# A cross-attention block on one core: output-projection products 1 and 7 split once more into 128x128 products, and the work of the other engines redistributed

## The chip, the cores and the metric

The kernel runs on 1 core of one Trainium2 chip. The metric is the time of one execution on the device in microseconds (us); the median of several runs is compared. Names of the engines in the profile: PE is TensorE (PEld its weight loads), DVE is VectorE, ACT is ScalarE, POOL is GpSimd, SP is SyncE, which issues most transfers (SPq is its queue). Each engine works off its own instructions strictly in the order of the program, and waits where an operand or a buffer is not ready.

## What is computed

A cross-attention block with adaptive layer norms, all in float32: 16 batches of 1024 query rows and 64 context rows, 512 features, 16 heads of 32. Cut to what matters:

```
ss    = silu(cond) @ W_ss + b_ss               # one scale and one shift per batch
xq    = (1 + scale_q) * layernorm(x)   + shift_q
xkv   = (1 + scale_kv) * layernorm(ctx) + shift_kv
q     = xq @ Wq + bq;   k, v = split(xkv @ Wkv + bkv)
attn  = softmax(q k^T / sqrt(32))              # per head, over 64 context rows
out   = x + (attn v) @ Wp + bp
```

## The kernel before, in words

The 1024 query rows of each batch make two tiles of 512 rows, 32 tiles in all (`NB`), numbered through. The context of all batches is projected once, at the start, as two groups "A" and "B" of 512 rows. The order of every step is written out by hand: a start, a loop `for i in range(3, NB - 2)` (L1587 to L1704), and an end. One loop body holds work of five tiles at once: scores of tile i, the softmax's rest and the mix of a = i-1, the output projection of b = i-2 and a, the query projection of n = i+1, and the features of f = i+2, i+3 and i+4.

**The steps of one tile.** `load_x` brings 512 rows; `q_stats` (L315) takes mean and variance of each row on VectorE (bn_stats and bn_aggr), four row blocks a tile; `q_scale` makes 1/std on ScalarE and POOL; `hidden` normalises on ScalarE (L327); `turn` (L352) transposes 32x32 blocks on VectorE and `move` (L373) brings them to their partitions by 16 transfers of 64 KB; `scale_features` applies scale and shift on ScalarE (L442).

**Seven products.** Both projections multiply 512x512 by 512x512 with Strassen's scheme in Winograd's form: seven products of halves (numbers 1 to 7; 256x256 by 256x256 here, each four matmuls of 128 columns by 256) in place of eight, with sums of halves made beforehand on POOL (`feature_sums` L474, `row_sum` L1046) and the results added up in two PSUM banks and by VectorE (`query_added` L647, `added` L1095). Product 1, 6, 5 and 3 gather in one bank and 2 or 7 and 4 in the other; each is read before the next is added, so the products of a bank follow each other with a reader in between. For the query projection of tiles 4 to 30 products 1 and 7 are split once more: `quarter_products` (L585) multiplies seven pairs of 128x128 quarters, four (`first`) and then three, with differences of quarters made on POOL (`feature_quarters` L578), a copy by ScalarE (`quarter_copies` L614) and three sums by VectorE between the two parts (`quarter_adds` L618). The sums of weight quarters are made once.

**Softmax.** `score_products` (L731) writes the scores of 32 context rows (half z) into two PSUM tiles of two banks each. The tag "s" has two such buffers, so both halves of a tile's scores and the mix of another tile (L919) take the same four banks in turn. `maximum` (L754) reduces a bank pair on VectorE, `copied` (L763) copies it to SBUF on ScalarE, `maxima` (L789) joins the halves and spreads the maximum over the partitions by a VectorE transpose, `subtract` (L795) takes it off on POOL, and `weights` (L803) exponentiates on ScalarE. So that the mix can use 64 context rows per matmul, half the blocks of 32 partitions must change places between the two halves: `swapped` (L810) moves two of the four by transfer, and `again` (L815) exponentiates the other two once more from the scores. `total` (L851) adds the two halves on POOL, `row_total` (L861) sums the rows on VectorE. `inverse_rows` (L875) takes the reciprocals and brings them by way of DRAM into an order from which `spread_rows` (L886) spreads them on VectorE with a 2048-wide transpose. `mix` (L919) multiplies by the values, and `divided` (L898) multiplies the result in PSUM by the spread reciprocals.

**Output projection.** `biased` (L1019) puts the bias into a bank on ScalarE, `output_seed` (L1035) copies product 1's bank to the other, `product` (L1064) runs one of the seven products, `added` adds to the residual rows and, after products 3 and 4, stores them. Tile 29 alone is projected undivided, by `project` (L971). At the very end tile 31 uses halves of banks of its own.

Of the kernel before, what the change touches and what calls it, by code (L numbers as in the profile page):

```python
# [9 lines left out]
F32 = mybir.dt.float32  # L10
# [10 lines left out]
def cross_attention_block(  # L21
# [166 lines left out]
    def load_projection(again=False):  # L188
        src = w_p.rearrange("(c p) o -> p c o", p=P)
        if again:  # L190
            nc.sync.dma_start(w_p_sb[:, : NC // 2, H // 2 :], src[:, : NC // 2, H // 2 :])
        else:
            nc.sync.dma_start(w_p_sb, src)

    ident = const.tile([P, P], F32, name="ident")
# [67 lines left out]
    def scale_shift(name, off, h, n=1):  # L263
        rows = ssr.pop((name, h))
        pst = pss_tiles[name][1]
        if h == 0:
            ss[name] = const.tile([P, 2 * NC, BW], F32, name=f"ss_{name}")
# [47 lines left out]
    def q_stats(i, ts=range(NT)):  # L315

        if ts[0] == 0:
            q_mv[i] = small.tile([P, NT, 2], F32, tag="mvq", name=f"mvq_{i}")
        for t in ts:
            row_stats(q_mv[i][:, t, :], x_tiles[i][:, t, :])  # L320

# [409 lines left out]
    def score_products(i, z):  # L731
# [13 lines left out]
        if z == 0:  # L745
            m_tiles[i] = small.tile([P, 2, HPC, NJ], F32, tag="m2", name=f"m2_{i}")
# [51 lines left out]

    l_tiles = {}
# [14 lines left out]

    def again(i, g):  # L815
# [7 lines left out]
    def sums(i, z):  # L823
        if z == 0:
            l_tiles[i] = small.tile([P, 2, HPC, NJ], F32, tag="l2", name=f"l2_{i}", bufs=1)
# [35 lines left out]
    def row_total(i):  # L861
        lt_tiles[i] = small.tile([P, HPC, NJ], F32, tag="lt", name=f"lt_{i}", bufs=2)
# [8 lines left out]
    def halves_total(i):  # L871
        lt_tiles[i] = small.tile([P, HPC, NJ], F32, tag="lt", name=f"lt_{i}", bufs=2)
        both(lt_tiles[i].rearrange("p r j -> p (r j)"), l_tiles.pop(i), ALU.add)

    def inverse_rows(i):  # L875
# [3 lines left out]
        v = small.tile([P, NC, NJ], F32, tag="vr", name=f"vr_{i}", bufs=2)  # L879
# [4 lines left out]
        vt_rows[i] = v  # L884

# [125 lines left out]
    def acc_bank(i, n):  # L1011

        if n == 2 and i >= NB - 2:
            return 1 if i == NB - 2 else 3
        return (2 if n in (1, 6, 5, 3) else 3) - (2 if i == NB - 1 else 0)
# [3 lines left out]
    def biased(i, k):  # L1019

        b = b_first if k == 2 else b_diff
        if i == NB - 1 and k == 2:
            z_halves.append(bank(f"pp_{i}_0", 0))
            z_halves.append(ps_s.tile([P, 2, TB], F32, tag="s", name=f"pp_{i}_0b")[:, 0, :])
# [10 lines left out]
    def output_seed(i):  # L1035

        seeded.add((i, 2))
        acc[3] = bank(f"pp_{i}_2", 3)
        nc.scalar.copy(acc[3], acc[2])
# [24 lines left out]
    def product(i, n):  # L1064
# [12 lines left out]
        if n == 2 and (i, 2) not in seeded:  # L1077
            acc[k] = bank(f"pp_{i}_{n}", k)
        for t in range(2):
            for c in range(HC):  # L1080
# [12 lines left out]
                )  # L1093

# [29 lines left out]
    w_k_sums = big.tile([P, 4, HC, HO], F32, tag="big2", name="w_k_sums")  # L1124
    warm = bank("warm", 1)
    for _ in range(WARM):
        nc.tensor.transpose(warm[:, :P], ident, ident)
    load_x("A")
    load_scale_shift("kv", w_ss_kv, 0)
    q_stats("A", (0,))  # L1130
    q_stats("A", (1,))
    q_stats("A", (2,))
    load_scale_shift("kv", w_ss_kv, 1)
    q_stats("A", (3,))
    q_scale("A")
    load_context_weights(1, 0)
    hidden("A", (0,))
    biases()
    load_context_weights(0, 1)
    scale_shift_rows("kv", 0)  # L1140
    scale_shift_taken("kv", 0)
    turned_features("A", 0)
    hidden("A", (2,))
    hidden("A", (1,))
    turned_features("A", 1)
    hidden("A", (3,))
    scale_shift("kv", 2 * NC, 0)
    turned_features("A", 2)
    turned_features("A", 3)
    modulated("A", 0, 1, nc.vector)  # L1150
    load_context_weights(0, 0)
    modulated("A", 0, 0, nc.scalar)
    scale_shift_rows("kv", 1)
    scale_shift_taken("kv", 1)
    load_x(0)
    modulated("A", 0, 0, nc.vector)
    modulated("A", 0, 1, nc.scalar)
    load_scale_shift("q", w_ss_q, 0)
    column_sums("k", w_k_sb, w_k_sums, (0,))
    scale_shift("kv", 2 * NC, 1)  # L1160
    load_scale_shift("q", w_ss_q, 1)
    column_sums("k", w_k_sb, w_k_sums, (1,))
    modulated("A", 1, 0, nc.scalar)
    column_sums("k", w_k_sb, w_k_sums, (2,))
    modulated("A", 1, 0, nc.vector)
    context_product("A", "v", 1)
    context_product("A", "k", 2)
    modulated("A", 1, 1, nc.vector)
    load_x("B")
    modulated("A", 1, 1, nc.scalar)  # L1170
    feature_sums("A", nc.vector, (0,))
    context_product("A", "k", 1)
    feature_sums("A", nc.vector, (1,))
    context_out("A", "k", 1)
    feature_sums("A", nc.vector, (2,))
    q_stats(0, (0,))
    context_out("A", "k", 2)
    context_product("A", "v", 2)
    context_product("A", "k", 6)
    q_stats(0, (1,))  # L1180
    q_stats(0, (2,))
    scale_shift_rows("q", 0)
    q_stats(0, (3,))
    q_scale(0)
    context_out("A", "k", 6)
    feature_sums("A", nc.vector, (3,))
    hidden(0, (1,))
    hidden(0, (2,))
    hidden(0, (0,))
    load_context_weights(1, 1)  # L1190
    load_value_bias()
    w_q_sums = qpool.tile([P, 4, HC, HO], F32, tag="wq", name="w_q_sums")
    context_product("A", "k", 7)
    load_query_weights()
    context_out("A", "k", 7)
# [12 lines left out]
    column_sums("v", w_v_sb, wv_sums, (0,))
# [660 lines left out]
```

## Time and profile before

| | |
|---|---|
| runs | 998.51, 998.59, 996.92 us; median 998.51 |
| profiled execution | 996.92 us, its span 996.9 us |
| granted TensorE clock | 1.000 |
| DMA | 165.77 MB, mean 166 GB/s |
| HBM | 79.47 MB read, 34.60 MB written |

The span runs from the first to the last instruction. Busy shares are shares of the span; a matmul's end is modelled and matmuls overlap, so the pace of TensorE is read from start to next start. In lists of instructions, "x8" are eight instructions: a float32 matmul appears as two passes. "[0.65 <-PE po L936]" says that the engine had been idle for 0.65 us until the named instruction of another engine released it.

### The profile page before, as it was taken

Reading aid. Unit: us, or ns where it says so; the run is one execution under the profiler, and the core shown is the slowest. Engines: PE = TensorE matmul, PEld = TensorE weight load, DVE = VectorE, ACT = ScalarE, POOL = GpSimd, SP = SyncE. Lnnn points to the kernel's source line nnn. Section 1 sums busy time; section 2 is a strip of 40 time slices with the busy share of each in tenths; the row PEclk is TensorE's granted clock in tenths of the full one; section 3 lists DMA queues with packets and bytes.
Section 4 is the critical chain, followed back from the end, with each engine's and each line's share of the span. In section 5 each row is a group of like instructions: output and inputs, shape, how many; then the busy total and the mean of one; then the engine's idle time right before and its main releaser. Section 6 shows DMA issues by size and latency. Waiting matters only on the chain.

```text
span 996.9 us, 20564 instructions
## 1 busy us (share of the span) xinstructions
PE 984.2 (99%) x7465; PEld 760.7 (76%) x7465; DVE 895.6 (90%) x1318; ACT 779.3 (78%) x1165; POOL 895.4 (90%) x690
## 2 busy tenths in 40 slices
PE   7999999999999999999999999999999999999998
PEld 6878777787777877877778778777787787777756
DVE  7696899999999999999999999999999999987786
ACT  3878878888888888888888888888888888876620
POOL 2677899999999999999999999999999999999681
PEclk9999999999999999999999999999999999999999
DMA  9765655555655555566655555665555555544422
GB/s 308 264 165 151 156 164 156 140 165 180 190 181 176 159 165 152 151 182 186 183 176 152 173 145 155 185 188 178 176 150 175 151 154 182 148 132 130 145 85 97
DMA packets 115188, 165.77 MB, mean 166 GB/s; under 512 B 34920, under 2 KB 46464, under 8 KB 113168
## 3 DMA queue, kind: packets, MB, share of 16 engines
q1 hardware_dynamic: 114704, 163.93, 55.2%
q8 instruction: 59, 0.97, 0.4%
q0 software_dynamic: 384, 0.54, 0.2%
q14 instruction: 41, 0.34, 0.1%
HBM read 79.47 MB, written 34.60 MB: 114 GB/s over the span
## 4 chain that ended last, share of the span: by engine, by line
PE 88%; DMA 4%; DVE 3%; SPq 2%; POOL 1%; issue 1%; ACT 0%; DVEq 0%; POOLq 0%
PE pp L1086 36%; PE pq L534 27%; PE pq L605 10%; PE ps L738 6%; PE po L936 5%; PE pk_A L534 1%; PE pk_B L534 1%; DMA w_k_sb<-in_L_xcond_Wkv_dram 1%; DMA r<-in_x_dram 1%; PE pv_B L534 1%; DMA ltd<-lt 1%; DMA V_B<-stage_B 1%; DMA vr<-ltd 0%; POOL sum L858 0%; DVE l L826 0%
## 5 line engine op out<-in xcount | busy, mean ns | idle before, releaser
L797 POOL TENSOR_TENSOR s<-s,mb 128x2048 f32<-128x2048 f32 x64 | 290.6, 4564 | 20.3 <-DVE mb L784 13.4
L1086 PE MATMUL pp<-w_p_sb,ot 128*128 128x256 f32 x740 | 174.8, 379 | 1.1 <-DVE ot L915 1.1
L764 ACT COPY s<-ps 128x1024 f32<-128x1024 f32 x128 | 129.3, 1013 | 46.1 <-PE ps L738 34.0
L755 DVE TRANSPOSE_TENSOR_REDUCE m<-ps 128x32 f32<-128x1024 f32 x128 | 152.4, 1228 | 10.4 <-PE ps L738 9.3
L1086 PEld LDWEIGHTS pp<-w_p_sb,ot 128*128 128x128 f32 x740 | 138.2, 190 | 20.5 <-issue 2.8
L645 ACT ACTIVATE qt<-pq,bias_t 128x256 f32<-128x256 f32 x256 | 107.8, 475 | 48.8 <-PE pq L605 27.7
L858 POOL TENSOR_TENSOR sum<-s,p 128x2048 f32<-128x2048 f32 x30 | 136.5, 4549 | 1.6 <-ACT p L808 1.6
L1116 DVE TENSOR_TENSOR r<-pp,r 128x512 f32<-128x512 f32 x183 | 120.3, 669 | 13.8 <-ACT xt L442 6.8
L534 PE MATMUL pq<-xt,w_q_sums 128*128 128x256 f32 x512 | 123.8, 385 | 0.0
L534 PEld LDWEIGHTS pq<-xt,w_q_sums 128*128 128x128 f32 x512 | 95.0, 190 | 34.6 <-issue 22.6
L1086 PE MATMUL pp<-WT,ot 128*128 128x256 f32 x492 | 118.4, 383 | 0.0
L1086 PE MATMUL pp<-WT,s 128*128 128x256 f32 x488 | 116.1, 380 | 1.3 <-DVE r L1107 0.8
L817 ACT ACTIVATE s<-s 32x2048 f32<-32x2048 f32 x60 | 114.6, 1910 | 1.8 <-DMA p<-s 0.4
L1086 PEld LDWEIGHTS pp<-WT,ot 128*128 128x128 f32 x492 | 90.9, 190 | 19.1 <-issue 4.2
L1086 PEld LDWEIGHTS pp<-WT,s 128*128 128x128 f32 x488 | 88.2, 190 | 13.1 <-POOL s L1056 1.3
L327 ACT ACTIVATE x<-x,rstdq 128x512 f32<-128x512 f32 x128 | 94.8, 807 | 1.0 <-POOL rstdq L304 1.0
L442 ACT ACTIVATE xt<-xt,ss_q 128x512 f32<-128x512 f32 x124 | 94.0, 809 | 1.0 <-DMA xt<-ht 0.7
L915 DVE TENSOR_TENSOR ot<-po,vb 128x1024 f32<-128x1024 f32 x62 | 73.0, 1219 | 17.6 <-PE po L936 17.4
L286 DVE BATCH_NORM_STATS2 bs<-x 128x6 f32<-128x512 f32 x128 | 85.3, 666 | 0.0
L493 POOL TENSOR_TENSOR xt_sums<-xt 128x512 f32<-128x512 f32 x64 | 81.2, 1269 | 2.0 <-DMA x<-in_x_dram 1.3
L357 DVE STREAM_TRANSPOSE ht<-x 128x512 f32<-128x512 f32 x124 | 77.7, 679 | 4.7 <-DMA xt<-ht 2.2
L891 DVE STREAM_TRANSPOSE vb<-vr 128x2048 f32<-128x2048 f32 (+1 forms) x33 | 73.7, 2236 | 4.4 <-DMA vr<-ltd 4.4
(224 smaller groups left out, 1963.8 us busy)
## 6 DMA issues: line engine op xcount, KB each, us to landing
x<-in_x_dram SPq DMA_DIRECT2D x32, 1024.0 KB, 5.3
r<-in_x_dram SPq DMA_DIRECT2D x32, 1024.0 KB, 5.9
xt<-ht SPq DMA_DIRECT2D x488, 64.0 KB, 2.0
out_dram<-r SPq DMA_DIRECT2D x60, 512.0 KB, 4.7
p<-s SPq DMA_DIRECT2D x60, 256.0 KB, 3.8
wss_kv<-in_L_xcond_Wss_kv_dram SPq DMA_DIRECT2D x4, 512.0 KB, 7.2
wss_q<-in_L_xcond_Wss_q_dram SPq DMA_DIRECT2D x4, 512.0 KB, 11.0
vr<-ltd SPq DMA_DIRECT2D x128, 8.0 KB, 1.7
```

Source lines behind the costliest of these rows:

```text
L327: nc.scalar.activation(dst, src, AF.Identity, bias=rstd[:, 1, j : j + 1], scale=rstd[:, 0, j : j + 1])
L442: nc.scalar.activation(xt[:, :, c, :], xt[:, :, c, :], AF.Identity, scale=ss["q"][:, c, b : b + 1], bias=ss["q"][:, NC + c, b : b + 1],)
L534: nc.tensor.matmul(out_, lhsT=lhsT, rhs=rhs, start=new and m == 0 and c == 0, stop=c == HC - 1, skip_group_check=True,)
L605: nc.tensor.matmul(qa["q", k][:, q * P : (q + 1) * P], lhsT=lhsT, rhs=rhs, start=first and q == 0, stop=True, skip_group_check=True,)
L645: nc.scalar.activation(dst, src, AF.Identity, bias=bq_t[:, o : o + 1])
L755: nc.vector.tensor_reduce(m_tiles[i][:, z, 2 * e : 2 * e + 2, :], s_banks[i, z][e].rearrange("p r (j a) -> p r j a", a=32), AX.X, ALU.max, ...
L764: nc.scalar.copy(s_tiles[i, z][:, 2 * e : 2 * e + 2, :], s_banks[i, z][e])
L797: eng.tensor_tensor(s_tiles[i, z], s_tiles[i, z], mb_tiles[i], ALU.subtract)
L817: nc.scalar.activation(s_tiles[i, 0][at + 32 : at + 64], raw_tiles[i][at : at + 32], AF.Exp, scale=SCALE)
L858: nc.gpsimd.tensor_tensor(t, s_tiles[i, 0], s_tiles[i, 1], ALU.add)
L1086: nc.tensor.matmul(to, lhsT=rows[:, c, t * P : (t + 1) * P], rhs=cols[:, c, :], start=n == 2 and (i, 2) not in seeded and t == 0 and c == ...
L1116: nc.vector.tensor_add(r, a, r)
```

## The change

**Split products of the output projection.** Products 1 and 7 of tiles 2 to 30, and product 7 of tile 31, become seven products of 128x128 quarters, in the same way as the query projection's, with new functions:

```diff
+    def inner_biased(i, v):
+
+        k = acc_bank(i, v)
+        acc[k] = bank(f"pp_{i}_{k}", k)
+        nc.scalar.copy(acc[k][:, :HO], inner_bias[v])
+        nc.scalar.copy(acc[k][:, HO:], zero.to_broadcast([P, HO]))
...
+    def inner_quarters(i, v, eng=nc.gpsimd):
...
+        x, tt = inner_rows(i, v), eng.tensor_tensor
+        tt(t[:, 0:2], x[:, 1, 0:2, :], x[:, 0:2, 0, :], ALU.subtract)
+        tt(t[:, 2], x[:, 1, 1, :], t[:, 0], ALU.subtract)
+        tt(t[:, 3], x[:, 0, 1, :], t[:, 2], ALU.subtract)
+
+    def inner_products(i, v, first):
...
+        if first:
+            todo = (
+                (0, w(0, 0), x[:, 0, 0, :]),
+                (2, s(0), t[:, 0]),
+                (1, s(2), t[:, 1]),
+                (3, s(1), t[:, 2]),
+            )
+        else:
+            todo = (
+                (0, w(0, 1), x[:, 0, 1, :]),
+                (2, s(3), x[:, 1, 1, :]),
+                (1, w(1, 1), t[:, 3]),
+            )
...
+    def inner_copies(i, v):
+        a = acc[acc_bank(i, v)].rearrange("p (k e n) -> p k e n", k=2, e=2)
+        nc.scalar.copy(inner_tiles[i, v][:, 0:2], a[:, :, 0, :])
+
+    def inner_adds(i, v):
+
+        a, t, tt = acc[acc_bank(i, v)], inner_tiles[i, v], nc.vector.tensor_tensor
+        both_ = a[:, P : 3 * P].rearrange("p (k n) -> p k n", k=2)
+        tt(t[:, 2], a[:, 3 * P :], t[:, 0], ALU.add)
+        tt(both_, both_, t[:, 2:3].to_broadcast([P, 2, P]), ALU.add)
+        tt(a[:, 3 * P :], a[:, P : 2 * P], t[:, 1], ALU.add)
```

The weight quarters' sums are made once (`inner_weight_sums`), one of them in place, so `load_projection(again=True)` now reads 512 KB back, late in the end, where it read 256 KB earlier in it. Tile 29 uses the seven products too, and `project` is not called any more. Tile 31's query products 1 and 7 are split.

**Softmax.** For tiles 3 to 30 the second half's scores are not copied to SBUF and not lowered by POOL: `lowered` subtracts the maximum on VectorE straight from the score banks, which stay taken until then. For tiles 2 to 29 `exchanged` moves all blocks by six transfers of 256 KB, and `again` is gone. For tiles 2 to 30 the reciprocals are transposed (64 wide), written to DRAM and read back already spread, by four broadcast reads of 256 KB, and `spread_rows` is gone:

```diff
+    def lowered(i, e):
+        rs = slice(2 * e, 2 * e + 2)
+        nc.vector.tensor_tensor(
+            s_tiles[i, 1][:, rs, :], s_banks[i, 1][e], mb_tiles[i][:, rs, :], ALU.subtract
+        )
...
+    def exchanged(i, k):
...
+        t = raw_tiles[i]
+        for g in range(2):
+            lo, hi = slice(64 * g, 64 * g + 32), slice(64 * g + 32, 64 * g + 64)
+            dst, src = ((t[lo], s0[hi]), (t[hi], s1[hi]), (s0[hi], s1[lo]))[k]
+            nc.sync.dma_start(dst, src)
...
+    def reciprocal_rows(i):
...
+        nc.vector.reciprocal(flat, flat)
+        nc.vector.transpose(v.rearrange("p k a -> p (k a)"), flat)
+        nc.sync.dma_start(d.rearrange("k x a -> x k a"), v)
...
+    def read_rows(i, rs=range(HPC)):
...
+        for r in rs:
+            src = vt_rows[i][r // 2].rearrange("(c k j) a -> k c (j a)", c=NC, k=2)
+            src = src[r % 2 : r % 2 + 1].to_broadcast([32, NC, TB])
+            nc.sync.dma_start(vb_tiles[i][32 * r : 32 * r + 32], src)
```

**Row statistics.** For tiles 7 to 31 two of the four row blocks get their mean and variance on ScalarE, in two passes with an accumulator each, and POOL divides the squares by 512:

```diff
+    def q_stats_two(i, ts, last=False):
...
+            nc.scalar.activation(junk, x, AF.Identity, scale=1.0 / H, accum_out=mv[:, t, 0:1])
+            nc.scalar.activation(
+                junk, x, AF.Square, scale=-1.0, bias=mv[:, t, 0:1], accum_out=mv[:, t, 1:2]
+            )
```

**The order.** All of it is written anew. The loop now runs `for i in range(5, NB - 4)`, 23 bodies, and its body starts at another point of the cycle. Its calls in order, with the guards that always hold or hold until the last tiles left out:

```
query_out(i,6); maxima(a); product(i-3,3); scale_features(n,2); quarter_products(i,7,first);
product(i-3,4); scale_features(n,0); lowered(a,0); lowered(a,1); quarter_copies(i,7);
added(i-3,3); quarter_adds(i,7); weights_whole(a,1); mix(b); turn(f,0); subtract(a,0);
added(i-3,4); inner_biased(b,1); weights(a,0); quarter_products(i,7,second); turn(f,1);
feature_quarters(n,1); divided(b,0); inner_quarters(b,1); exchanged(a,0); query_product(i,5);
divided(b,1); inner_products(b,1,first); query_out(i,7); total(a); turn(f,2); load_residual(a);
turn(f,3); q_stats_two(i+3,0); query_added(i,5); inner_copies(b,1); exchanged(a,1);
row_sum(b,0); inner_adds(b,1); query_product(i,4); query_product(i,3); scale_features(n,3);
q_stats_two(i+3,1); query_out(i,3); move(f,0); inner_products(b,1,second); row_sum(b,2);
query_added(i,4); output_seed(b); q_stats(i+3,2); q_stats(i+3,3); score_products(i,0);
copied(i,0,1); row_sum(b,1); q_square_mean(i+3); exchanged(a,2); product(b,2); row_total(a);
maximum(i,0,0); quarter_products(n,1,first); added(b,2); inner_quarters(b,7);
quarter_copies(n,1); move(f,1); reciprocal_rows(a); feature_sums(n,0); maximum(i,0,1);
product(b,6); load_x(i+4); inner_biased(b,7); inner_products(b,7,first); move(f,2);
copied(i,0,0); q_scale(i+3); feature_sums(n,1); quarter_adds(n,1); feature_sums(n,2);
added(b,6); move(f,3); read_rows(a,0:2); score_products(i,1); read_rows(a,2:4);
quarter_products(n,1,second); inner_copies(b,7); product(b,5); feature_sums(n,3);
inner_adds(b,7); hidden(i+3,0); inner_products(b,7,second); query_seed(n); query_product(n,2);
hidden(i+3,3); maximum(i,1,0); feature_quarters(n,7); query_product(n,6); maximum(i,1,1);
added(b,7); hidden(i+3,2); hidden(i+3,1); row_sum(b,3); query_out(n,2); added(b,5);
scale_features(f,1)
```

At the start, the loads are issued in the order context A, x of tile 0, both parts of the scale and shift weights for keys and values, then the key weights of the first half, a half of the value weights and the other key weights (before: context A, the scale and shift weights, the value weights' half, the key weights' halves the other way round, and then x of tile 0), and the first product on TensorE is the key product 1 instead of the value product 1. The tiles 28 to 31 are written out one by one at the end.

A few small tiles lose a buffer or share one with another (`lt`, `vr` and `m2`, the identity matrix's place), and the statistics' scratch and product 7's quarter tile take the place of the spread maximum (tag "spread").

More of the change, by code (lines that the diff above doesn't have):

```diff
@@ L1076, in product @@
         k = acc_bank(i, n)
-        if n == 2 and (i, 2) not in seeded:
+        if n == 2 and (i, 2) not in seeded and k < 4:
             acc[k] = bank(f"pp_{i}_{n}", k)
@@ new lines, in cross_attention_block @@
+    subtract(3, zs=(0,))
+    product(1, 3)
+    weights_whole(3, 1)
+    query_product(4, 5)
+    inner_weight_sums(1)
+    inner_weight_sums(7)
+    quarter_products(4, 7, False)
+    mix(2)
+    feature_quarters(5, 1)
+    q_stats_two(7, (0,))
+    added(1, 4)
+    query_out(4, 7)
+    added(1, 3)
+    query_added(4, 5)
+    query_product(4, 3)
+    query_product(4, 4)
+    divided(2, (0,))
+    q_stats_two(7, (1,))
+    inner_biased(2, 1)
+    inner_quarters(2, 1)
+    weights(3, 0)
+    divided(2, (1,))
@@ new lines, in cross_attention_block @@
+    q_stats_two(31, (0,))
+    quarter_adds(28, 7)
+    turn(30, (0,))
+    product(25, 3)
+    added(25, 3)
+    turn(30, (1,))
+    product(25, 4)
+    turn(30, (2,))
+    quarter_products(28, 7, False)
+    added(25, 4)
+    mix(26)
+    divided(26, (0,))
+    query_product(28, 5)
+    query_out(28, 7)
+    divided(26, (1,))
+    q_stats_two(31, (1,))
+    query_added(28, 5)
+    turn(30, (3,))
+    feature_quarters(29, 1)
+    inner_quarters(26, 1)
+    load_residual(27)
+    inner_biased(26, 1)
@@ new lines, in cross_attention_block @@
+    query_out(30, 6)
+    quarter_adds(30, 7)
+    product(27, 4)
+    added(27, 3)
+    lowered(29, 1)
+    lowered(29, 0)
+    added(27, 4)
+    query_product(30, 5)
+    scale_features(31, (3,))
+    quarter_products(30, 7, False)
+    query_out(30, 7)
+    query_added(30, 5)
+    subtract(29, zs=(0,))
+    weights_whole(29, 1)
+    mix(28)
+    feature_sums(31, nc.gpsimd, (0,))
+    feature_quarters(31, 1)
+    inner_biased(28, 1)
+    weights(29, 0)
+    query_product(30, 3)
+    divided(28, (0,))
@@ L1730, in cross_attention_block @@
+    read_rows(29, (2, 3))
+    quarter_adds(z, 7)
+    weights(y, 1)
+    weights(y, 0)
+    quarter_products(z, 7, False)
+    query_out(z, 7)
+    query_added(z, 5)
+    load_residual(NB - 1)
+    added(y - 2, 4)
+    mix(y - 1)
+    divided(y - 1, (0,))
+    divided(y - 1, (1,))
+    total(y)
     query_product(z, 4)
-    query_added(z, 5)
     query_product(z, 3)
-    product(y - 2, 5)
-    again(y - 1, 1)
+    query_out(z, 3)
+    inner_biased(y - 1, 1)
     query_added(z, 4)
-    added(y - 2, 7)
```

1697 lines of the change are left out of this document (1104 added, 593 removed).

## The prediction

> **What bounds the kernel now.** I read the page, then the busy time by stretches, then each engine's timeline over one tile, then the ends.
>
> ```profile
> span 996.9 us, 20564 instructions
> PE 984.2 (99%) x7465; PEld 760.7 (76%) x7465; DVE 895.6 (90%) x1318; ACT 779.3 (78%) x1165; POOL 895.4 (90%) x690
> ```
> ```profile
> 0.00:25.00 25.00, 18.92 (x158) 16.20 (x159) 17.55 (x49) 9.41 (x24) 7.43 (x13) 1.00 0.95 308
> ...
> 200.00:228.30 28.30, 28.30 (x220) 21.95 (x219) 26.76 (x40) 24.26 (x37) 27.57 (x22) 1.00 0.61 182
> ...
> 960.00:997.00 37.00, 31.68 (x186) 23.18 (x184) 26.98 (x33) 5.12 (x5) 12.41 (x8) 0.99 0.30 108
> ```
> The columns of a stretch are its length, then PE, PEld, DVE, ACT and POOL busy, the granted clock, the DMA share and GB/s. TensorE is never idle in the middle; of its 12.7 us of idle time (996.9 less 984.2) 6.1 lie in the first 25 us and 5.3 in the last 37. So the time moves only by TensorE work taken away, or by new idle time. But POOL with 27.57 and DVE with 26.76 of 28.30 stand right behind it. The timelines give the pace, start to next start, which is shorter than a row's own duration because operations overlap:
>
> ```profile
> 501.05 1.89 PE L534 MATMUL pq<-xt,w_q_sb 128*128 128x256 f32 x8
> ...
> 504.51 0.38 PE L605 MATMUL pq<-xt_sums,w_q_sums 128*128 128x128 f32 x2
> 504.73 0.83 PE L605 MATMUL pq<-t_quarters,w_p_sb 128*128 128x128 f32 x6
> 505.40 1.89 PE L1086 MATMUL pp<-w_p_sb,ot 128*128 128x256 f32 x8
> 507.13 1.89 PE L1086 MATMUL pp<-WT,ot 128*128 128x256 f32 x8
> ...
> 529.57 1.89 PE L534 MATMUL pq<-xt,w_q_sb 128*128 128x256 f32 x8
> ```
> A plain product is 8 passes in 1.73 us (505.40 to 507.13). Four quarter products are 8 passes in 0.89 us (504.51 to 505.40), 0.111 a pass, so seven of them, 14 passes, take 1.56. One tile takes 28.52 us (501.05 to 529.57).
>
> **TensorE's work.** Products 1 and 7 of the output projection are split for tiles 2 to 30 and 2 to 31: 59 in all, 57 of them outside tile 29, each 1.73 less 1.56 = 0.17: 9.5 us. The query products 1 and 7 of tile 31 give 0.3. Tile 29 loses its undivided projection:
>
> ```profile
> 947.68 7.11 PE L974 MATMUL pp<-w_p_sb,ot 128*128 128x512 f32 x16 [0.33 <-PE ps L738]
> 954.72 2.35 PE L947 MATMUL po<-s,V_B 32*32 32x512 f32 x64
> 957.00 7.13 PE L974 MATMUL pp<-w_p_sb,ot 128*128 128x512 f32 x16
> 963.97 3.62 PE L1086 MATMUL pp<-w_p_sb,ot 128*128 128x256 f32 x16
> ```
> That was 7.04 + 6.97 = 14.0; five plain and two split products take 8.65 + 3.12 = 11.8, so 2.2 less. TensorE loses 12.0 us, and a tile of the loop falls from 28.52 to 28.18.
>
> **VectorE.** One tile of its timeline:
>
> ```profile
> 491.72 2.31 DVE L863 TRANSPOSE_TENSOR_REDUCE lt<-sum 128x64 f32<-128x2048 f32 x1
> ...
> 494.89 2.39 DVE L755 TRANSPOSE_TENSOR_REDUCE m<-ps 128x32 f32<-128x1024 f32 x2 [0.27 <-PE ps L738]
> ...
> 501.55 2.31 DVE L784 STREAM_TRANSPOSE mb<-m 128x2048 f32<-128x2048 f32 x1
> 503.79 0.65 DVE L1116 TENSOR_TENSOR r<-pp,r 128x512 f32<-128x512 f32 x1
> 504.36 0.67 DVE L286 BATCH_NORM_STATS2 bs<-x 128x6 f32<-128x512 f32 x1
> ...
> 505.17 0.66 DVE L286 BATCH_NORM_STATS2 bs<-x 128x6 f32<-128x512 f32 x1
> ...
> 506.54 0.28 DVE L622 TENSOR_TENSOR t_quarters<-pq,t_quarters 128x128 f32<-128x128 f32 x1
> ...
> 507.53 2.30 DVE L891 STREAM_TRANSPOSE vb<-vr 128x2048 f32<-128x2048 f32 x1
> 509.75 1.25 DVE L1116 TENSOR_TENSOR r<-pp,r 128x512 f32<-128x512 f32 x2
> 511.65 2.36 DVE L915 TENSOR_TENSOR ot<-po,vb 128x1024 f32<-128x1024 f32 x2 [0.65 <-PE po L936]
> 513.92 2.48 DVE L357 STREAM_TRANSPOSE ht<-x 128x512 f32<-128x512 f32 x4
> ...
> 520.23 2.31 DVE L863 TRANSPOSE_TENSOR_REDUCE lt<-sum 128x64 f32<-128x2048 f32 x1
> ```
> Of the 28.51 from L863 to L863 it waits 0.27 + 0.65 = 0.92 and works at most 27.59. Removed: the spreading of the reciprocals (L891, 2.22) and two of four row statistics (0.81 each). Added: two `lowered`, which read a score bank and an SBUF tile as L915 does (2.27 for two), two `inner_adds`, each like L622 to L624 (0.99), and a 64-wide transpose (L784 does 2048 in 2.24, so 0.1 in proportion, at most 0.3). Sum: 27.59 - 2.22 - 1.62 + 2.27 + 1.98 + 0.1 = 28.1. Against TensorE's 28.18 next to nothing is left, where 0.92 was: this is what decides the change.
>
> The pace matters here. The Trainium skill ("VectorE: DVE Perf Modes", section The DRAIN you can't avoid) says that the next operation does not start until the pipe of the one before is empty. By that rule, the trace disagrees: L1116 lasts 0.65 and L286 starts 0.57 after it.
>
> **The other engines.**
>
> ```profile
> 501.92 0.74 POOL L581 TENSOR_TENSOR t_quarters<-xt_sums 128x256 f32<-128x256 f32 x1
> ...
> 504.01 9.08 POOL L797 TENSOR_TENSOR s<-s,mb 128x2048 f32<-128x2048 f32 x2 [0.27 <-ACT qt L645]
> 513.05 1.28 POOL L1051 TENSOR_TENSOR s<-ot 128x512 f32<-128x512 f32 x1
> ```
> ```profile
> L764 ACT COPY s<-ps 128x1024 f32<-128x1024 f32 x128 | 129.3, 1013 | 46.1 <-PE ps L738 34.0
> L645 ACT ACTIVATE qt<-pq,bias_t 128x256 f32<-128x256 f32 x256 | 107.8, 475 | 48.8 <-PE pq L605 27.7
> L817 ACT ACTIVATE s<-s 32x2048 f32<-32x2048 f32 x60 | 114.6, 1910 | 1.8 <-DMA p<-s 0.4
> L327 ACT ACTIVATE x<-x,rstdq 128x512 f32<-128x512 f32 x128 | 94.8, 807 | 1.0 <-POOL rstdq L304 1.0
> ```
> POOL gives up one subtraction (4.52) and gets two sets of quarter differences (501.92 to 503.74, 1.82 each): 0.9 less with one tiny product. ScalarE drops two score copies (2.0) and the two second exponentials of `again` (3.8), and gets four passes of statistics as long as L327 (3.2; the accumulator is not in the trace, 0 to 0.3 each, I take 0.1) and small copies (0.8): 1.5 less. Neither can become the bound; both keep their order, so the question there is only lateness.
>
> SP and the DMA queues get more:
>
> ```profile
> q1 hardware_dynamic: 114704, 163.93, 55.2%
> ...
> p<-s SPq DMA_DIRECT2D x60, 256.0 KB, 3.8
> ...
> b_p_sb<-in_L_xcond_bp_dram SPq DMA_DIRECT2D x1, 256.0 KB, 6.5
> ```
> Per tile, four more exchanges of 256 KB and four broadcast reads of 256 KB in place of four small ones: 2 MB, 58 MB over the kernel. 163.9 MB take 55.2% of the queue engines, so 222 MB would take 75%: not the bound, but transfers land later. An exchange landed in 3.8 us; a broadcast read of the same size in 6.5, and I take 4 to 6.5. The last exchange waits on SP for POOL's `total`, as `swapped` did; behind it stand feature moves, and what it brings is used a tile later. The reads stand behind 8 feature moves:
>
> ```profile
> 493.56 8.28 SPq L382 DMA_DIRECT2D xt<-ht  x11
> ```
> At 0.75 each these are 6.0, with the other issues 8.5, so the last read lands at most 8.5 + 6.5 = 15.0 after the reciprocals. Its first user, `divided`, comes after 15.5 us of VectorE's queue (three maxima 3.5, two `quarter_adds` and one `inner_adds` 3.0, five residual sums 3.0, `maxima` 2.6, `lowered` 2.3, two transposes 1.2): it fits by 0.5, or by 3 at 4 us a read. `lowered` itself waits for nothing new but `maxima`, ahead of it in the same queue; behind it stand a residual sum and `quarter_adds`, for which TensorE has 2 us more.
>
> **Three tight places of the new loop,** each TensorE against the chain it waits for. (1) The mix takes the score banks only after `lowered`. TensorE does 10.9 us in between (two second halves of a split product, 0.67 each, one first half, 0.89, five plain products, 8.65); VectorE needs 0.27 + 2.4 (two maxima) + 1.2 (two residual sums) + 2.57 (`maxima`) + 2.27 = 8.7. 2.2 are left, or 1.2 with an `inner_adds` in front. (2) From the mix to the first inner products TensorE has 0.67 + 1.73 = 2.4; the chain is 0.16 + 1.2 (`divided`, one half) + 0.82 (the first quarter difference, L581 with its gap) = 2.2. 0.2 are left. (3) The scores need both halves of `query_out` of product 3, 0.2 + 0.84 (two L645, overlapping), while only 0.67 of inner products lie between, where before a whole product of 1.73 did. 0.3 short if all scores wait for both halves, 0 if the first column of scores starts on the first half; I take 0.05 a tile, near the lower end, since the scores walk through the columns one after the other. Over 23 loop bodies this is 1.2 us, with 0 to 7 as its bounds.
>
> **The ends.** At the start 1 MB (x of tile 0) goes ahead of the scale and shift weights:
>
> ```profile
> 10.75 1.07 PE L248 MATMUL ps_kv<-wss_kv,early 128*32 128x128 f32 x28 [0.99 <-DMA wss_kv<-in_L_xcond_Wss_kv_dram]
> ...
> 19.24 3.69 PE L534 MATMUL pk_A<-xk_A,w_k_sb 128*128 128x256 f32 x16 [1.42 <-DMA w_k_sb<-in_L_xcond_Wkv_dram]
> ```
> At 308 GB/s that is 3.4 us on a TensorE that waits for these weights already; but the first key product then needs 4.5 MB ahead of it, as it did before, so it starts again near 19, and only the value product that ran before it comes later: +1.0 (bounds -1 to +3.4). The half of the projection weights that is read again comes before the last mix and has several microseconds of cover. At the end TensorE had 5.3 idle; the last products still hang on the same mix and the same stores, so 0, with bounds of 1.5 either way.
>
> **The sum.** The profiled execution took 996.92 us, as its span does, and is the lowest of the three runs; the median 998.51 is 1.6 above it. 996.9 - 12.0 + 1.2 + 1.0 = 987.1, and 988.7 as a median.
>
> **Rivals.** (a) Short stalls eat most of the gain: 0.2 to 0.4 more per tile at places 2 and 3, over 25 tiles 5 to 10 us: 994 to 999. For it speaks the 0.2 of room; against it, that TensorE shows no idle time in the loop with POOL as full as it is. (b) VectorE becomes the clock, the slower case: it keeps the 0.92 of waits on top of 28.1, 29.0 a tile against 28.18, over 25 tiles +20: 1009. It decides as soon as its waits pass 0.1 to 0.2 a tile; against it, the waits come from VectorE being early for the scores and the mix, and a later VectorE waits less, while place 1 has room for a VectorE one microsecond later. Late reads of the reciprocals would end the same way: 2 us beyond their room put 2 us on each tile. (c) The operations of VectorE do not overlap: 40 instructions in the stretch of 28.30 with about 0.05 of overlap each are 2 us more, 30.1 a tile, +48: 1037. The old tile would then have been 29.6 instead of 28.51, so 1 in 100. This is what the rule of the Trainium skill cited above would make of the change. (d) The split brings no time because the order outside the loop loses what it gives, an end that costs 8 us or more: 997, with only 1 in 25, as the ends hold just 11 us of idle time and are built of the same waits.
>
> **Numbers.** Forecast 0.67 (984 to 993), (a) 0.14, (b) 0.14, (c) 0.01, (d) 0.04. Two in a thousand, 2.0 us, is about what can be told from no change. Faster (below 996.5): 0.67 and two thirds of (a), 0.76; same: the rest of (a) and (d), 0.09; slower: (b) and (c), 0.15. The range takes in the forecast's own bounds and (a): 984 to 1000.
>
> **What would show it.** Right: PE busy near 972, still 99%; a loop tile of 28.2 to 28.3; the split product's seven in 1.56; DVE at 27.6 to 28.1 a tile with waits under 0.5. Place 3 would show as PEld waiting on `qt`, place 2 as PE waiting on POOL's quarter tile, the reads as DVE waiting for a transfer into `vb`. Wrong: a tile of 28.5 or more with PE idle behind DVE, or a start in which TensorE idles over 8 us.

## The result and the profile after

The changed kernel takes 1141.43 us (median of four runs, 1139.02 to 1143.58) against 998.55 before (four runs, 996.92 to 999.48). The ratio is 1.1434, with a 95% interval of 1.1415 to 1.1453. The change makes the kernel 143 us slower; the forecast was 988.7 us, in a range of 984 to 1000.

The page of the profiled execution (1141.46 us): the span, the busy times, the DMA queue, and three rows of the DMA issues (KB each, median us from issue to landing).

```profile
span 1139.7 us, 22368 instructions
...
PE 1027.8 (90%) x7855; PEld 803.5 (71%) x7855; DVE 919.9 (81%) x1457; ACT 717.7 (63%) x1377; POOL 877.7 (77%) x881
...
q1 hardware_dynamic: 123760, 223.02, 72.7%
...
x<-in_x_dram SPq DMA_DIRECT2D x32, 1024.0 KB, 6.5
...
xt<-ht SPq DMA_DIRECT2D x488, 64.0 KB, 4.8
p<-s SPq DMA_DIRECT2D x116, 256.0 KB, 4.8
```

No engine is full any more: TensorE falls from 99% of its span to 90%, and VectorE and POOL fall too. So no engine has become the clock; they wait for one another. Stretches of the same trace (length, PE, PEld, DVE, ACT, POOL busy, granted clock, DMA share, GB/s):

```profile
0.00:25.00 25.00, 18.61 (x147) 16.13 (x148) 16.25 (x53) 9.92 (x28) 5.50 (x12) 0.93 0.94 303
...
300.00:900.00 600.00, 539.41 (x4201) 425.28 (x4200) 501.39 (x781) 396.98 (x779) 479.29 (x493) 0.96 0.79 208
...
1100.00:1139.00 39.00, 34.60 (x247) 28.47 (x232) 29.66 (x45) 7.97 (x13) 18.93 (x17) 1.00 0.36 122
```

In the 600 us of loop TensorE idles 60.6 us and its granted clock is 0.96, where before it was never idle and at 1.00. Taking the start of a tile's first score products as a mark, the 142.8 us (1139.7 less 996.9) lie as follows: up to tile 5 the mark moves from 208.4 to 231.9 (+23.5); from tile 5 to tile 27 the loop takes 726.9 instead of 627.4 (+99.5; 33.04 us a tile instead of 28.52, irregular, 30 to 37); from there to the end 180.9 instead of 161.1 (+19.8).

Who waits for whom, in the groups of waits over the whole kernel (us in total, times, longest):

```profile
ACT xt L459 <- DMA xt<-ht: 122.8, 25, 8.2
DVE t_quarters L639 <- ACT t_quarters L633: 97.4, 22, 8.1
...
PE pq L622 <- DVE pq L641: 66.9, 23, 6.7
```

These three are one chain, once a tile. One stalled tile shows it, first SP's queue, then ScalarE, VectorE and TensorE:

```profile
508.82 0.49 SPq L119 DMA_DIRECT2D x<-in_x_dram  x1
509.35 8.15 SPq L399 DMA_DIRECT2D xt<-ht  x8
517.55 2.04 SPq L948 DMA_DIRECT2D vb<-ltd  x4
```
```profile
519.17 0.81 ACT L459 ACTIVATE xt<-xt,ss_q 128x512 f32<-128x512 f32 x1 [8.11 <-DMA xt<-ht]
...
522.01 0.36 ACT L633 COPY t_quarters<-pq 128x256 f32<-128x256 f32 x1
```
```profile
522.47 0.29 DVE L639 TENSOR_TENSOR t_quarters<-pq,t_quarters 128x128 f32<-128x128 f32 x1 [7.09 <-ACT t_quarters L633]
```
```profile
517.01 1.06 PE L1002 MATMUL po<-p,V_A 64*32 64x512 f32 x16
523.71 0.77 PE L622 MATMUL pq<-xt_sums,w_q_sums 128*128 128x128 f32 x2 [5.64 <-DVE pq L641]
...
525.12 2.67 PE L551 MATMUL pq<-xt,w_q_sums 128*128 128x256 f32 x8
```

The last eight feature moves stand right behind the 1 MB load of x. They take SP 8.15 us, but not evenly. It issues seven of them 0.63 us apart, and the eighth only at 517.00 (the same timeline in two narrower windows):

```profile
509.35 4.36 SPq L399 DMA_DIRECT2D xt<-ht  x7
...
517.00 0.51 SPq L399 DMA_DIRECT2D xt<-ht  x1
```

In all traces of this case SP's transfers carry eight semaphores in turn (a semaphore is the counter by which a landed transfer reports), and no transfer was issued before the one eight places ahead of it, which carried the same semaphore, had landed, wherever the records tell the landing. Eight places ahead of the eighth move stands the x load, which landed at 516.98. Eight places ahead of the second transfer of the third exchange (L852) stands the residual load. SP's own groups of waits from tile 5 to tile 27 show both:

```profile
SPq L852 <- DMA r<-in_x_dram: 54.8, 21, 3.7
SPq L399 <- DMA x<-in_x_dram: 41.9, 22, 3.4
```

Neither wait is there in the loop of the kernel before. The seven moves issued at once land late as well: they come in right behind the load, between 517.27 and 518.33, and the eighth at 518.91.

`scale_features(f, (1,))`, which needs them, is the head of ScalarE's queue for the next body, and behind it stand `query_out(i, 6)` and the copies of a split query product (L633). VectorE's `quarter_adds` waits for those copies, and TensorE for the sums. TensorE then resumes at a lower clock: eight passes take 2.67 us instead of 1.89. The granted clock in that place, by stretches:

```profile
511.00:517.00 6.00, 6.00 (x44) 4.66 (x51) 4.34 (x4) 0.06 (x1) 6.00 (x3) 1.00 0.84 244
517.00:523.70 6.70, 1.07 (x24) 0.17 (x9) 1.09 (x4) 4.53 (x7) 0.01 (x2) 0.97 0.76 174
523.70:526.70 3.00, 2.99 (x10) 2.73 (x11) 3.00 (x5) 2.97 (x5) 1.65 (x3) 0.50 0.72 267
526.70:533.00 6.30, 6.30 (x39) 5.53 (x42) 6.06 (x14) 5.37 (x15) 6.12 (x5) 1.00 0.75 176
```

After a 5.64 us pause the clock is 0.50 for the next 3.0 us, which costs 3.0 × 0.50 = 1.5 us on top of the pause. Over the 600 us, 0.04 of clock is about 24 us and the idle time 60.6: together about 85, and the 18.2 tiles of this stretch are 18.2 × 4.52 = 82 us longer than before. So the loss in the loop is pauses and the low clock behind them.

### The profile page after: what moved, and what is told of

The parts are those of the page before. It is cut to its first block, busy times and chain, and to the rows that moved or that the text cites. A ratio compares the mean times of both kernels' runs of the same rounds, so it can differ in the third digit from the quotient of the medians.

```text
span 1139.7 us, 22368 instructions
## 1 busy us (share of the span) xinstructions
PE 1027.8 (90%) x7855; PEld 803.5 (71%) x7855; DVE 919.9 (81%) x1457; ACT 717.7 (63%) x1377; POOL 877.7 (77%) x881
## 3 DMA queue, kind: packets, MB, share of 16 engines
q1 hardware_dynamic: 123760, 223.02, 72.7%
## 4 chain that ended last, share of the span: by engine, by line
DMA 33%; PE 22%; DVE 15%; ACT 10%; POOL 8%; SPq 8%; issue 4%; DVEq 0%; ACTq 0%; POOLq 0%
DMA x<-in_x_dram 16%; PE pq L551 8%; DMA vb<-ltd 5%; DMA p<-s 5%; POOL sum L902 4%; SPq L399 4%; PE pp L1155 4%; DVE m L772 3%; DMA xt<-ht 3%; ACT xt L459 3%; PE pp L1246 2%; PE pq L622 2%; DVE lt L907 2%; DVE r L1288 2%; DVE ot L981 2%
## 5 line engine op out<-in xcount | busy, mean ns | idle before, releaser
L459 ACT ACTIVATE xt<-xt,ss_q 128x512 f32<-128x512 f32 x124 | 97.3, 810 | 138.0 <-DMA xt<-ht 122.8
L814 POOL TENSOR_TENSOR s<-s,mb 128x2048 f32<-128x2048 f32 x36 | 163.6, 4547 | 12.4 <-DVE mb L801 12.3
L902 POOL TENSOR_TENSOR sum<-s,s 128x2048 f32<-128x2048 f32 x29 | 131.8, 4544 | 2.3 <-ACT s L836 2.2
L1155 PE MATMUL pp<-w_p_sb,ot 128*128 128x256 f32 x524 | 128.2, 388 | 5.1 <-ACT pp L1108 3.8
L1155 PEld LDWEIGHTS pp<-w_p_sb,ot 128*128 128x128 f32 x524 | 95.5, 191 | 38.8 <-ACT pp L1108 23.6
L639 DVE TENSOR_TENSOR t_quarters<-pq,t_quarters 128x128 f32<-128x128 f32 x56 | 15.2, 272 | 99.1 <-ACT t_quarters L633 97.4
L781 ACT COPY s<-ps 128x1024 f32<-128x1024 f32 x72 | 72.1, 1012 | 36.4 <-PE ps L755 24.1
L598 POOL TENSOR_TENSOR t_quarters<-xt 128x256 f32<-128x256 f32 x28 | 20.6, 737 | 91.1 <-DVE pq L641 53.7
L622 PE MATMUL pq<-xt_sums,w_q_sums 128*128 128x128 f32 x112 | 25.9, 316 | 66.9 <-DVE pq L641 66.9
L622 PEld LDWEIGHTS pq<-xt_sums,w_q_sums 128*128 128x128 f32 x112 | 20.8, 207 | 89.9 <-issue 84.1
L801 DVE STREAM_TRANSPOSE mb<-m 128x2048 f32<-128x2048 f32 x32 | 74.0, 2311 | 1.2
```

The lines of the kernel that those rows point to most:

```text
L459: nc.scalar.activation(xt[:, :, c, :], xt[:, :, c, :], AF.Identity, scale=ss["q"][:, c, b : b + 1], bias=ss["q"][:, NC + c, b : b + 1],)
L814: eng.tensor_tensor(s_tiles[i, z], s_tiles[i, z], mb_tiles[i], ALU.subtract)
L902: nc.gpsimd.tensor_tensor(t, s_tiles[i, 0], s_tiles[i, 1], ALU.add)
L1155: nc.tensor.matmul(to, lhsT=rows[:, c, t * P : (t + 1) * P], rhs=cols[:, c, :], start=n == 2 and (i, 2) not in seeded and t == 0 and c == ...
```

## The experiments

Each time is that of one execution, beside one of the kernel before (998.4, 997.5 and 998.2 us in three groups); only e12 is a median of four. Executions of the changed kernel lie up to 5 us apart (1139.0 to 1143.6), so smaller differences in the time say nothing. Theories, with the letters that the expectations use. **H**: an in-order queue holds up what stands behind a late item, SP's first and then ScalarE's. **B**: the 2 MB more a tile make every transfer late, in whatever order. **V**: VectorE has become the clock (rival (b) of the prediction). Later, **Q** narrows H to SP: what is late is what SP has behind the two 1 MB loads, x and residual; **L**: behind the x load alone.

| run | us | the edit | us a tile, 5 to 27 |
|---|---|---|---|
| e1_load_later | 1085.7 | x load behind the row reads | 30.6 |
| e2_scale_later | 1123.0 | scalings later on ScalarE | 32.2 |
| e3_spread_back | 1204.1 | reciprocals the old way, 1 MB less a tile | 35.7 |
| e4_no_split | 1131.9 | products 1 and 7 undivided | 32.9 |
| e5_residual_later | 1077.8 | residual load behind the row reads | 30.2 |
| e6_both_later | 1054.2 | e1 and e5 | 28.9 |
| e7_both_scale | 1058.7 | e6 and e2 | 29.3 |
| e8_both_exch | 1072.0 | e6, third exchange behind the moves | 29.7 |
| e9_all_later | 1038.8 | e6, the same at both ends | 28.8 |
| e10_before_residual | 1007.3 | the old kernel, residual load early | 29.0 |
| e11_later_no_split | 1055.1 | e6 and e4 | 29.4 |
| e12_products_swapped | 1040.0 | e9, query products 3 and 4 exchanged | 28.8 |

**e1_load_later.**
```
         read_rows(a, (2, 3))
+        load_x(i + 4)        # was ahead of inner_biased(b, 7) and the last eight moves
```


> In the loop the 1 MB load of x for tile i+4 is issued after the last broadcast read instead of ahead of the feature moves. Theory H (head of line: the last eight moves stand behind this load in the transfer queues, the scaling at the end of the loop body waits for them on ScalarE, and everything behind it in ScalarE's order waits too, up to the quarter products): ScalarE's wait for the moves falls from 122.8 us to under 30, the time to 1010 to 1050. Theory B (the 2 MB more per tile load the transfer engines too much): the bytes are the same, so 1110 to 1150. Theory V (VectorE has become the clock): 1130 to 1150.

1085.69 us, 56 less than after. The moves land in 3.1 us (median of all, 4.8 after), and ScalarE's wait for them, in the groups of waits, falls from 122.8 but does not go:
```profile
ACT xt L459 <- DMA xt<-ht: 75.7, 25, 5.4
```
The direction is H's, the size was not (1010 to 1050, with a wait under 30). Something else was still ahead of the moves, and SP's own groups of waits name the residual load: 71.4 us for the store that it waits for (L126) and 36.3 for its landing (L852).

**e2_scale_later.**
```
-        scale_features(n, (2,)); scale_features(n, (0,)); scale_features(f, (1,))
         quarter_copies(i, 7)
+        scale_features(n, (1,)); scale_features(n, (2,)); scale_features(n, (0,))
```


> In the loop the three scalings that need the moves stand on ScalarE behind the query output of product 6 and the quarter copies, instead of ahead of them; no transfer is moved. Theory H: TensorE's 66.9 us of waiting for the quarter sums mostly go, though the moves land as late as before, and the time falls to 1020 to 1070. Theory B: the lateness comes back at the next user of the features, 1110 to 1150. Theory V: 1130 to 1150.

1123.04 us, a miss for H's number: only 18 less. It lies in the range of B, which also said that the lateness would come back at the next user, so this run by itself does not tell H from B. With nothing waiting at the head of ScalarE the lateness shows at the next reader, the broadcast reads that stand behind the moves:
```profile
DVE ot L981 <- DMA vb<-ltd: 60.4, 21, 4.3
ACT xt L459 <- DMA xt<-ht: 30.9, 15, 6.4
```
So ScalarE's order mostly chooses where the wait appears. The cause is ahead of it, in the transfers.

**e3_spread_back.**
```
-        reciprocal_rows(a); read_rows(a, (0, 1)); read_rows(a, (2, 3))
+        inverse_rows(a)      # and spread_rows(b) behind lowered(a, 1)
```


> In the loop the reciprocals go the old way (small transfers and a 2048-wide transpose on VectorE), so 1 MB per tile less is transferred and VectorE has 2.2 us per tile more. Theory H: the reads stand behind the moves, so the moves land as late as before: 1120 to 1170. Theory B: half of the added bytes are gone, 1040 to 1080. Theory V: slower than the changed kernel, 1180 to 1200.

1204.05 us, outside all three ranges, and the slowest of all with the fewest bytes (DMA share 0.60 from 300 to 900 us). That speaks against B, though the order changed too. It is near V's number, but VectorE is busy only 498.4 of those 600 us. The old way puts SP to wait for its own store before it can read back, ahead of the moves; how much of the loss is this wait and how much the 2.2 us more of VectorE was not separated. In the groups of waits, SP's own and then ScalarE's:
```profile
SPq L927 <- DMA ltd<-lt: 37.5, 26, 3.1
```
```profile
ACT xt L459 <- DMA xt<-ht: 184.8, 25, 10.2
```

**e4_no_split.** The quarters, copies and sums of products 1 and 7 are left out, and the products are computed whole.
```
 def inner_products(i, v, first):
+    return product(i, v) if first else None
```


> Products 1 and 7 of the output projection are undivided again, everything else as in the changed kernel: VectorE has 2 us, POOL 3.6 us and ScalarE 0.8 us per tile less to do, TensorE 0.33 more. Theory H: the order of transfers and of ScalarE is the same, 1120 to 1150. Theory B: the same, 1120 to 1150. Theory V: 1010 to 1060, as VectorE is relieved.

1131.87 us. V falls: with 2 us a tile less of VectorE (866 us busy instead of 920) and 3 less of POOL the kernel gains 10 us, 3 of them in the loop, and ScalarE still waits 112.8 us for the moves.

**e5_residual_later.**
```
         read_rows(a, (2, 3))
+        load_residual(a)     # was between exchanged(a, 0) and exchanged(a, 1)
```


> From the changed kernel, in the loop only the load of the residual rows is moved, from behind the first exchange (where its buffer is still being stored, so that SP waits for the store) to the end of the body's transfers. Theory Q (SP's order: what matters is how long SP stands still ahead of the moves): SP's waits for stores and loads shrink, the moves are issued 2 to 4 us earlier, 1070 to 1110. Theory L (only the 1 MB load right ahead of the last eight moves matters): 1130 to 1150. Theory B (bytes): 1130 to 1150.

1077.79 us, 64 less than after: no less than moving the x load, and in Q's range. L falls.

**e6_both_later.** Both edits.

> Both 1 MB loads (x of tile i+4 and the residual rows) stand behind the last broadcast read in the loop. Theory Q: the loop comes down to about 28.5 to 29.3 us a tile, the time to 1035 to 1055, the rest of the loss being outside the loop. Theory L: as with the load of x alone, 1080 to 1090. Theory B: the load on the transfer engines does not change, 1080 or more.

1054.15 us, as Q said, and 87 less than after (less than the 56 and 64 of the two edits alone added up). The wait falls to a third, and the loop is nearly that of before. SP waits in it for the landing of neither load. ScalarE's group of waits, a stretch of the loop, and SP's timeline of one tile:
```profile
ACT xt L459 <- DMA xt<-ht: 36.1, 21, 5.9
```
```profile
300.00:800.00 500.00, 496.52 (x3988) 392.58 (x3987) 475.61 (x739) 379.25 (x741) 456.43 (x467) 1.00 0.86 236
```
```profile
501.70 4.94 SPq L399 DMA_DIRECT2D xt<-ht  x8
506.69 2.03 SPq L948 DMA_DIRECT2D vb<-ltd  x4
508.76 0.43 SPq L119 DMA_DIRECT2D x<-in_x_dram  x1
509.24 0.51 SPq L126 DMA_DIRECT2D r<-in_x_dram  x1
```
The same bytes a tile now run at 236 GB/s instead of 208, with a DMA share of 0.86 instead of 0.79, and TensorE is busy 496.5 of 500 us: the transfer engines were not the bound, and B falls. The eight moves take SP 4.94 us instead of 8.15, now all of them 0.62 to 0.63 apart.

**e7_both_scale and e8_both_exch.** On top of e6, the scalings later on ScalarE (as e2), or:
```
         move(f, ks=(3,))
+        exchanged(a, 2)      # was ahead of product(b, 2)
```


> Both loads behind the reads, and the three scalings behind the quarter copies on ScalarE. Theory Q with ScalarE's head of line: no wait of TensorE for the quarter sums is left, 28.2 to 28.8 us a tile, 1030 to 1045. Theory L: 1075 to 1085. Theory B: 1080 or more.

> Both loads behind the reads, and the last exchange, for which SP waits for POOL's total, behind the last moves. Theory Q: the moves no longer stand behind any wait but that for the query products, so ScalarE's wait for them falls below 10 us: 1030 to 1045. Theory L: 1080 to 1090. Theory B: 1080 or more.

1058.67 and 1071.95 us, two misses. e7 makes the tile regular, 29.3 us each (28.4 in the best tiles of e6), but `query_out` is now late behind the scalings, 0.74 us on average in 23 waits of TensorE:
```profile
PE pq L551 <- ACT qt L662: 17.0, 23, 3.6
```
In e8 ScalarE's wait for the moves does fall below 10 us (8.6), as expected, but the exchange comes late for its own reader:
```profile
DVE s L818 <- DMA s<-s: 28.3, 22, 2.4
```

**e9_all_later.** e6, and in the bodies written out ahead of and behind the loop:
```
+    load_x(3) ... load_x(7)  # each behind the last move of its body
+    load_residual(2), (3), load_x(8), load_residual(27), (29)   # each behind the row reads
```


> The whole change, with the loads behind the feature moves not only in the loop (as in the run at 1054 us) but also in the bodies written out ahead of it and behind it: each x load from tile 3 on stands behind the last move of the body, residuals 2, 3, 27 and 29 behind the row reads. Nothing is left out. Theory Q (the head of SP's queue: what stands behind a load or behind a wait for a store comes late): the run at 1054 still loses about 25 us up to the scores of tile 5 and 16 us at the end, and its moves behind the x loads of the start took 9.9 to 10.6 us of SP for eight; of the 25 some 10 to 18 should come back, so 1034 to 1046. Rival E (the ends lose by their new order on ScalarE, VectorE and GpSimd, not by SP): 1049 to 1056.

1038.76 us, in Q's range. Of the 55.5 us that e6's span has over the span before, 15.5 go: up to tile 5 the mark moves from 233.6 to 224.1, and from tile 27 on 178.4 remain of 183.0.

**e10_before_residual.** The old kernel, with one line of its loop moved:
```
         added(b, 3)
+        load_residual(i)     # was behind the last move
```


> The kernel before, with one edit in its loop: the residual load of a tile stands right behind the two output stores that read the same buffer, with the next x load, the exchange and the moves behind it, as in the kernel after. Nothing is left out. Theory Q1 (it is the short way from the moves to the scalings that makes the lateness cost: in the kernel before a tile's moves are scaled a tile later): 997 to 1003, with some 3 to 5 us a tile of SP waiting for a store and no wait of ScalarE for the moves. Theory Q2 (a wait for a store at the head of SP's queue stalls this kernel by itself): over 1010, with TensorE idle.

1007.3 us, between Q1 and Q2. The wait for the store is now at the head of SP's queue, and tiles of 29 to 30.2 us stand among those of 28.5:
```profile
SPq L126 <- DMA out_dram<-r: 88.6, 30, 4.2
```
ScalarE does not wait for the moves there, which are scaled a body later; it is the exchanges that come late (ACT L817 waits 21.8 us for `p<-s`). So the early residual load costs the old kernel 9 us by itself; in the new one its place was worth 64 (e5). That the difference comes from reading the moves in the same body is argued from this; no run changes that alone.

**e11_later_no_split.** e6 with products 1 and 7 undivided (left out as in e4).

> The kernel of the run at 1054 us (both loads behind the row reads in the loop), with projection products 1 and 7 undivided: their quarters, copies and sums are left out, and the products are computed whole, so TensorE has 0.17 us more a product by the rows. If the split pays as costed where no queue is late: 1061 to 1066, with a tile of 28.8 to 29.0 us. If place 3 of the prediction (scores 0.3 us short of the values of product 3) eats what it saves: 1052 to 1058, with a tile of 28.4 to 28.6. If VectorE and GpSimd, which the split loads with some 2 and 3 us a tile, hold the loop of that run back: below 1050.

1055.13 us, the time of the second answer, but each tile of the loop takes 29.4 us, which is none of the three. With nothing between query product 3 and the scores, TensorE waits longer there than in e6 (its timeline):
```profile
610.23 1.49 PE L755 MATMUL ps<-qt,K_B 32*32 32x512 f32 x32 [0.56 <-ACT qt L662]
```
28.52 + 0.56 + 0.35 (1.49 less 1.14) is 29.43. So with a clean SP queue the split does shorten the unstalled tile, from 29.4 to 28.4; e6 gives this back by its irregular tiles (28.9 on average) and at both ends.

**e12_products_swapped.** e9, and in the loop:
```
+        query_product(i, 3)  # ahead of query_product(i, 4)
+        query_added(i, 5)    # ahead of turn(f, (2,))
+        query_added(i, 4)    # behind q_stats(i + 3, (3,))
```


> The kernel of the run at 1038.8 us (all loads behind the moves), with place 3 of the prediction relieved in the loop: query product 3 stands ahead of product 4, so that its two passes through ScalarE are done before the scores begin, the sums of product 5 on VectorE stand ahead of two transposes, and the sums of product 4 behind the two statistics. Nothing is left out. If place 3 is what held the unstalled tile at 28.4 to 28.5 us (its first scores took 1.45 us and not 1.14): the scores of a tile take 1.14, an unstalled tile is 28.1 to 28.3, and the whole 1031 to 1036. Rival (another engine, VectorE at 28.1 a tile by the prediction, is the next clock, or the sums of product 4 are late in their turn): the tile stays at 28.4 or longer, and the whole at 1037 or above.

1040.02 us (four runs, 1039.08 to 1041.48; ratio to before 1.0425, interval 1.0400 to 1.0449). The rival held: the undisturbed tile is 28.6, against 28.4 in e9. In most tiles the first scores take 1.31 us instead of 1.45, so place 3 is relieved only in part. ScalarE is in time now, but VectorE is not, at two places (the group of waits from 300 to 800 us for the first; for the second the timeline of one of the worse tiles):
```profile
PEld pq L551 <- DVE qt L669: 3.3, 16, 0.3
```
```profile
626.39 0.72 DVE L669 TENSOR_TENSOR qt<-pq,qt 128x256 f32<-128x256 f32 x2
...
626.70 1.53 PE L755 MATMUL ps<-qt,K_B 32*32 32x512 f32 x32
...
627.17 0.15 PEld L755 LDWEIGHTS ps<-qt,K_B 32*32 32x32 f32 x8 [0.18 <-DVE qt L669]
```
The second sum of product 4 ends near 627.1, and the last eight passes of the scores wait for it. No version here beats the kernel before.

## Why the prediction was wrong

**The step that failed** is the one on the queues. It priced SP and DMA by bytes (75% of the queue engines, "not the bound, but transfers land later") and asked of lateness only whether the broadcast reads reach `divided`. It named the feature moves behind the third exchange and went on to what the exchange brings, not to who reads the moves. And it said of ScalarE and POOL that "neither can become the bound; both keep their order, so the question there is only lateness", without pricing that lateness. The bytes were right (223.0 MB, 222 said), and so nearly was the share (72.7%). What was missed is order: the new body issues `load_residual(a)` and `load_x(i + 4)` ahead of the moves, and reads the moves in the same body. The last moves land behind the x load, and through the eight semaphores SP stands still 96.7 us from tile 5 to tile 27 (54.8 + 41.9) until one or the other load has landed. The prediction put this term at nothing. Undoing these two lines in the loop gives back 87 of the 143 us (e6), and at the ends 15 more (e9).

The order before, which the prediction's fences do not show, kept both loads away from the moves:

```profile
492.95 8.89 SPq L382 DMA_DIRECT2D xt<-ht  x12
...
505.69 2.41 SPq L382 DMA_DIRECT2D xt<-ht  x4
508.15 0.58 SPq L126 DMA_DIRECT2D r<-in_x_dram  x1
...
516.47 0.38 SPq L119 DMA_DIRECT2D x<-in_x_dram  x1
520.22 1.15 SPq L813 DMA_DIRECT2D p<-s  x2
```

The residual load came behind all moves, and the x load 3.7 us ahead of the next small transfer; SP never waits in this loop for either load to land.

Rival (b) came nearest in kind, with its last sentence on late reads that put their delay on each tile. Its price, 1009 us, was for VectorE's own waits, and is 10 us of a loss of 143.

**TensorE's term** was right for each product (57 times 0.17 is 9.7 and not 9.5, which changes nothing). Three quarter products of the second half take 0.67 (507.56 to 508.23 in the trace after), as said. But the tile never reached 28.18. **Place 3** was mis-sized: taken as 0.05 a tile, it is 0.31, the upper of the two ends. From tile 5 to tile 27 of after, e6 and e9 the first scores take 1.45 us, in a few tiles up to 1.49, where they took 1.14 before. One tile of e9 shows both halves of the scores, and the weight loads of the first:

```profile
627.78 0.15 PEld L755 LDWEIGHTS ps<-qt,K_B 32*32 32x32 f32 x8
627.78 1.45 PE L755 MATMUL ps<-qt,K_B 32*32 32x512 f32 x32
...
628.11 0.21 PEld L755 LDWEIGHTS ps<-qt,K_B 32*32 32x32 f32 x24 [0.18 <-ACT qt L662]
...
634.60 1.14 PE L755 MATMUL ps<-qt,K_B 32*32 32x512 f32 x32
```

The first eight passes do start on the first half of `query_out`, as argued, but the other 24 wait for the second half until 628.11. So the best tile would be 28.18 + 0.31 = 28.49. The undisturbed tiles of e6 and e9 take 28.44, against 28.52 before: nearly all of the split's gain in the loop was gone before any transfer was late.

**VectorE** was sized well and was not what "decides the change". In e6 it is busy 475.6 of 500 us, 17.3 tiles: 27.5 a tile, where 27.6 to 28.1 was said; `lowered` takes 2.28 for two and `inner_adds` 0.99, as costed. e4 shows that 2 us a tile less of it bring 10 us. But in e12, where a chain needs its sums sooner, it is what the scores wait for. The prediction gives the rule of the Trainium skill ("VectorE: DVE Perf Modes", section The DRAIN you can't avoid) without what that section adds, that a next operation which is not held starts earlier; so the overlap that it found in the trace need not contradict the page. **POOL and ScalarE** were sized well too (26.4 and 21.9 a tile in e6).

**Places 1 and 2** held: in the kernel after no wait of the mix for `lowered` appears, and the inner products wait for POOL's quarters 3.3 us in all. **The reads** fit in the loop of e6, as said.

**The ends** were taken as +1.0 and 0. Behind e9, with the loads out of the way, they cost +15.7 up to tile 5 and +17.3 from tile 27, though the new order does two projection products, about 3.4 us of work, behind the mark of tile 5 instead of ahead of it; without this shift the figures are about 19.1 and 13.9. In these stretches lie many waits under 3 us of TensorE for ScalarE, VectorE and POOL, and low clock (0.95 up to 67.4 us). Both marks of a wrong forecast were met: a tile over 28.5 us with TensorE idle behind VectorE (which only passed the lateness on), and a start in which TensorE idles over 8 us (18.1 of the first 208 us, 208 less 189.88 busy; 7.1 in the kernel before). What each step of the new ends costs was not separated, and stays open. Of the residual load's price SP's waits tell a part: in the kernel after SP waits 12.7 us for the store ahead of it and 58.0 for its landing, over the whole span. How such waits of SP add up in TensorE's time is open, and no run changes the number of semaphores.

## What to carry to other kernels

Price an in-order DMA queue by its order, not only by its bytes: for each transfer write down what stands ahead of it (a load of a megabyte, a wait for a store), which transfer has to land before it is issued (here the one eight places ahead), and how long after its issue the first reader stands at the head of an engine's queue. In this kernel a transfer read in the same iteration had to be issued ahead of the large loads; one read an iteration later could stand behind them. And when a change shortens the work between a producer and its consumer, take the shortfall in full until a trace shows the overlap.

## What the runs showed of the hardware

Small transfers issued behind a megabyte load on the same queue land behind it: seven 64 KB moves, issued from 509.35 us on, landed between 517.27 and 518.33, and the load at 516.98. With both loads moved behind the moves (e6) the median from issue to landing fell from 4.8 to 2.7 us over the whole kernel (2.0 in the kernel before), and the DMA share and the throughput were higher. The Trainium skill ("DMA: Bandwidth & Descriptors", section Queues, rings and completion order) says that each DMA engine takes the descriptors of one queue in order. By that rule, the trace agrees.

SP's own pace did not change: 0.62 to 0.63 us a move in both orders. That eight moves took 8.15 us behind the load and 4.94 without is the eighth's wait for the load's landing, through the semaphore that the two share.

A TensorE pause of 5.6 us was followed by 3.0 us at a granted clock of 0.50; the waits of up to 0.6 us in the loops of e11 and e12 left it at 1.00. So a late transfer that causes a long pause is paid twice. The Trainium skill ("TensorE: Matmul & The Clock Gate", section Part 1: The HAM clock gate) says that the clock falls to half after an idle window of about 3.4 us and comes back after as long a busy one. By that rule, the trace agrees: 0.50 behind 5.64 us, and full speed 3.0 us later. No run here measured where the threshold lies. But below the page's figure both happened in the kernel after: pauses that ended at 357.8 and 623.1 us, 2.5 us each, left the clock at 1.00, and one of 2.2 us that ended at 389.8 was followed by 0.55 over 3.8 us, so a shorter pause can be enough.

A statistics pass on ScalarE carries a separate read of the accumulator, 0.19 us beside a pass of 0.63 to 0.72; the prediction took 0.1 for it.
